# One change to a graph layer: silu and exponentials on ScalarE by other functions, and three other ways to fetch sender rows

## The chip, the cores and the metric

The kernel runs on one core of one Trainium2 chip. The metric is the time of one execution on the device in microseconds. The engines are named as the profile names them: PE (TensorE, matmuls; PEld its weight loads), DVE (VectorE), ACT (ScalarE), POOL (GpSimd), SP (SyncE).

## The reference

One layer of a graph network with attention over all edges: 12500 nodes of 64 features, 412500 edges of 32 features, sorted by receiver.

```python
h = relu(layernorm(x))
msg_in = concat([h[src], h[dst], edge_attr], axis=-1)          # 160 wide
messages = silu(msg_in @ W1 + b1) @ W2 + b2                    # 64 wide
logits = silu(msg_in @ Wa1 + ba1) @ Wa2 + ba2                  # one per edge
att = softmax(logits, axis=0)                                  # over all edges
aggregated = segment_sum(messages * att, dst, num_segments=n)
out = x + silu(concat([h, aggregated]) @ Wu1 + bu1) @ Wu2 + bu2
```

## The kernel before

Head (node stage). `x` is normalised in chunks of 8 or 14 rows per partition; each chunk is transposed into the table `hT` in SBUF and multiplied by two weight blocks. The products are written to DRAM: `ts_d`, the sender table, and then `tr_d`, the receiver table, both 128 wide (64 for attention, 64 for the message), halved so that a tanh can make the silu.

Edge stage. Edges go in 403 groups (`g`) of 8 tiles of 128 edges (`K = 8`). Four groups are a batch for the softmax (fewer at the end). The softmax is kept running: each batch lowers a common maximum `nmax` and the sums so far are scaled. The program order on each engine is written out by hand (`pin`), and each engine works through its instructions in that order. One iteration of the loop over `g` does this:

- `begin(g)`: DVE adds the gathered sender rows `gs` to the receiver and edge part `pe` in PSUM (L553) and ACT takes the tanh of all 1024 columns (L556).
- `sum_up`: the softmax weights and sums of a group some five groups back: ACT copies the segment sums out of PSUM (`ss`, L632), `put` adds them to a table (L651, L655, L658), PE projects, `by_node` builds one-hot weights (`wt`, L620, eight instructions) and multiplies them with the messages.
- `burst`: for every second group from 8 on, one of the 8 tiles isn't gathered. ACT copies its 128 sender columns, four bytes each, out of `hT` at addresses held in registers (L483; the numbers are loaded with L479), 64 a group; PE multiplies that column block by a weight stack (L548), after L547 on DVE has cleared the wrong half.
- `load(g + 2)`: POOL issues 8 or 7 indirect gathers from `ts_d` (L513) into one of seven `gs` buffers. SP loads edge features, receiver numbers and a window of `tr_d` (L524, L527, L534); DVE compares (`eo`, L538) and PE makes `pe` (L542).
- `tile_bias`, in groups 17 to 113 twice in eight groups: PE multiplies a node block and DVE adds a bias (`bu`, L323).
- `end(g)`: DVE completes both silu halves as (tanh + 1) times the input (L566 for messages, L572 for attention), multiplies by `wa2` (L574) and sums (L577). At a batch's end `top` takes the maximum.
- `weigh`: in the first group of the next batch, DVE finds the new maximum (L603, L604, L606) and ACT takes two exponentials (L607, L610).

Behind the loop the sums are divided, the node update runs in 13 tiles and the result is stored.

Of the kernel before, what the change touches and what calls it, by code (L numbers as in the profile page):

```python
# [20 lines left out]
D = 64  # L21
# [21 lines left out]
HT_AT = 4224  # L43
ROUND = 12582912.0
WIDE = 128
EPS = 1e-5
# [11 lines left out]
def gnn_kernel(ctx: ExitStack, tc: tile.TileContext, n_edges, x, src, src_row, dst, dst_row, first, edge,  # L58
# [73 lines left out]
    with tc.tile_pool(name="node1", bufs=1) as node1, \  # L132
# [3 lines left out]

        sizes = [8] + [min(CB, NB - 16 - c) for c in range(0, NB - 16, CB)] + [8] if NB > 16 else [NB]
# [38 lines left out]
        pin(nc.scalar.activation(node1.tile([P, 1], F32, name="spare"), eps, AF.Sqrt))  # L176
        xms, sqs, rstds, hs, tss = ({} for _ in range(5))
# [5 lines left out]
        def subtract(i):  # L183

            n = chunks[i][1]
            total = node.tile([P, CB], F32, name="total")[:, :n]
            pin(nc.vector.tensor_reduce(total, xcs[i], AX.X, ALU.add))
            xm = xms[i] = node.tile([P, CB, D], F32, name="xm", bufs=3)[:, :n, :]
            pin(nc.vector.scalar_tensor_tensor(xm, total[:, :, None].to_broadcast([P, n, D]), -1.0 / D,
                                               xcs[i], op0=ALU.mult, op1=ALU.add))  # L190

        def square(i):
            n = chunks[i][1]
            sq = sqs[i] = node.tile([P, CB, D], F32, name="sq", bufs=3)[:, :n, :]
            pin(nc.scalar.activation(sq, xms[i], AF.Square))

        def totals(i):
            n = chunks[i][1]
            rstd = rstds[i] = node.tile([P, CB], F32, name="rstd")[:, :n]
            pin(nc.vector.tensor_reduce(rstd, sqs.pop(i), AX.X, ALU.add))  # L200
# [4 lines left out]
        def normal(i):  # L205
            n = chunks[i][1]
            rstd = rstds.pop(i)
            pin(nc.vector.reciprocal(rstd, rstd))
# [35 lines left out]
        nch = len(chunks)  # L244
# [22 lines left out]
        for c, nn in chunks:  # L267
# [92 lines left out]
def one_pass(tc, n_edges, v):  # L360
# [17 lines left out]
    with ExitStack() as ctx:  # L378
# [43 lines left out]
        with tc.tile_pool(name="work2", bufs=2) as work2, \  # L422
                tc.tile_pool(name="small", bufs=3) as small, \
                tc.tile_pool(name="pre_ps", bufs=AHEAD + 1, space=PSUM) as pre_ps, \
                tc.tile_pool(name="one_ps", bufs=1, space=PSUM) as one_ps:
            pes, gss, lgs, ps_, psums, sps, pps, ees, mts, nums, cols = ({} for _ in range(11))
# [12 lines left out]
            chosen = {g: i for i, g in enumerate(picks)}  # L439
            hT8 = v["hT"].rearrange("d b p -> d (b p)").bitcast(U8)  # L440
            sets = [(i, min(P, len(picks) - i)) for i in range(0, len(picks), P)]
# [3 lines left out]
            def places():  # L445
# [4 lines left out]
                for k, (i, n) in enumerate(sets):  # L450
                    e = (picks[i] * K + K - 1) * EP
                    nc.sync.dma_start(num[:n, k, :], bass.AP(
                        tensor=v["src_row"].tensor, offset=v["src_row"][:, e:].offset,
                        ap=[[EVERY * K * EP, n], [1, EP]]))
# [8 lines left out]
                for k, (i, n) in enumerate(sets):  # L463
                    nc.sync.dma_start(par_d[k * P:k * P + n, :], low[:n, k, :])
# [3 lines left out]
            def numbers(g):  # L468
                if g in chosen:
                    n = nums[g] = small.tile([P, EP], I32, name="half", bufs=3)  # L470
                    row = par_d[chosen[g]:chosen[g] + 1, :]
                    nc.sync.dma_start(n, bass.AP(tensor=row.tensor, offset=row.offset, ap=[[0, P], [1, EP]]))
                    cols[g] = small.tile([P, EP], F32, name="cols", bufs=3)

            def columns(g, first, n):
                if g not in chosen:
                    return
                to, i = cols[g].bitcast(U8), chosen[g]
                _, regs = nc.values_load_multi_w_load_instructions(  # L479
                    spots[i % P:i % P + 1, i // P, first:first + n], engines=[ENG.Activation],  # L480
                    min_val=HT_AT, max_val=HT_AT + 2 * NP - 4, skip_runtime_bounds_check_because=WHY)
                for i in range(n):
                    pin(nc.scalar.copy(to[:, 4 * (first + i):4 * (first + i) + 4],  # L483
                                       hT8[:, bass.ds(regs[i] - HT_AT, 4)]))

            def burst(g, k):
# [6 lines left out]
            tr_w = bass.AP(tensor=tr_d.tensor, offset=tr_d.offset,  # L493
                           ap=[[C, NP + WR - SHIFT], [SHIFT * C, 2], [1, C]])

            def registers(g, engine, at, base=base_sb, top=NP - 1):
                n = min(NQ, NG + (base is not base_sb) - g)
# [6 lines left out]
            def load(g):  # L504

                t = g * K
                if g % NQ == 0:
                    registers(g, ENG.SP, at_sp)
# [24 lines left out]
                for r in range(2):  # L533
                    nc.sync.dma_start(win[r * R:(r + 1) * R, :, r, :],  # L534
                                      tr_w[bass.ds(at_sp[g], R), :, :])
# [14 lines left out]
            def begin(g):  # L550

                n = K - (g in chosen)
                pin(nc.vector.tensor_tensor(gss[g][:, :n, :], pes[g][:, :n, :], gss[g][:, :n, :], ALU.add))  # L553
                if n < K:
                    pin(nc.vector.tensor_copy(gss[g][:, n, :], pes[g][:, n, :]))
                pin(nc.scalar.activation(pes[g], gss[g], AF.Tanh))  # L556

            def end(g, then=None):

                s = batch[g]  # L560
                if g == starts[s]:
                    lgs[s] = small.tile([EP, B * K], F32, name="lg")
                gs, th = gss.pop(g), pes.pop(g)

                def message():
                    pin(nc.vector.scalar_tensor_tensor(acts[g % ACTS][:, :, 0:U], th[:, :, U:C], 1.0,  # L566
                                                       gs[:, :, U:C], op0=ALU.add, op1=ALU.mult))

                if g < NG - 1:
                    message()  # L570
                att = th[:, :, 0:U]
                pin(nc.vector.scalar_tensor_tensor(att, th[:, :, 0:U], 1.0, gs[:, :, 0:U],  # L572
                                                   op0=ALU.add, op1=ALU.mult))
# [3 lines left out]
                pin(nc.vector.tensor_reduce(lgs[s][:, k:k + K], att, AX.X, ALU.add))  # L577
# [4 lines left out]
                if g == NG - 1:  # L582
                    message()

            def top(s):

                n = size[s] * K
                lg = lgs[s]
# [10 lines left out]
            def weigh(s):  # L599
# [5 lines left out]
                fall = small.tile([P, 1], F32, name="fall")  # L605
                pin(nc.vector.tensor_tensor(fall, nmax[:, s + 1:s + 2], nmax[:, s:s + 1], ALU.subtract))  # L606
                pin(nc.scalar.activation(scale[:, s:s + 1], fall, AF.Exp))  # L607
                p = ps_[s] = small.tile([EP, B * K], F32, name="p")
                psum = small.tile([EP, 1], F32, name="psum")
                pin(nc.scalar.activation(p[:, :n], lgs.pop(s)[:, :n], AF.Exp, bias=nmax[:EP, s + 1:s + 2],  # L610
                                         accum_out=psum))
                psums[s] = psum

            def by_node(g):
# [4 lines left out]
                for j in range(K):  # L619
                    pin(nc.vector.tensor_scalar(wt[:, j, :], iota_w[:EP, j // H, :],  # L620
                                                dloc[:, g * K + j:g * K + j + 1],
                                                p[:, k + j:k + j + 1],
                                                op0=ALU.is_equal, op1=ALU.mult))
# [94 lines left out]
            for g in range(NG):  # L718
# [6 lines left out]
                begin(g)  # L725
                if more and g < NG - 1:
# [10 lines left out]
                if g + AHEAD < NG:  # L737
                    load(g + AHEAD)
                numbers(g + 6)
# [384 lines left out]
```

## Time and profile before

| | |
|---|---|
| median of 3 runs | 3902.49 us (3900.42 to 3908.46) |
| profiled execution | 3904.89 us, span 3903.1 us |
| mean granted TensorE clock | 0.642 |
| indirect gathers on POOL | 3032, first at 51.7, last at 3846.0 us |
| byte copies on ACT | 24576, from 102.8 to 3711.6 us |
| DMA, mean | 100 GB/s |

Shares of busy time are means over head, loop and tail. Register, semaphore and DMA-issuing instructions aren't counted as busy, so an engine that loads register numbers between its instructions looks idle there, with "issue" as the reason.

### The profile page before, as it was taken

The page shows a single profiled execution, that of the slowest core. Times are in us where ns is not written, and L with a number is a line of the kernel's source. Part 1 is how long each engine was busy: PE and PEld are TensorE (multiplying, and loading weights), DVE is VectorE, ACT ScalarE, POOL GpSimd, SP SyncE. Part 2 cuts the span into 40 slices and gives each one's busy share as a digit, 9 for nine tenths or more (in the row PEclk, how much of TensorE's full clock was granted, in tenths as well). Part 3 has the DMA queues.
Part 4 walks back from the last instruction along what each step waited for, and adds up shares of the span by engine and source line. Part 5 has one row for each costly group of instructions (what it writes and reads, how often), then busy time and mean ns, then how long its engine had stood idle before and what let it go on. Part 6 is the DMA issues. An engine that isn't in the chain of part 4 may idle for free. (4 is left out here: it accounts for less than half of the span.)

```text
span 3903.1 us, 72226 instructions
## 1 busy us (share of the span) xinstructions
PE 2368.6 (61%) x11368; PEld 1927.2 (49%) x11368; DVE 3115.4 (80%) x8929; ACT 2954.1 (76%) x25797; POOL 2888.6 (74%) x3057
## 2 busy tenths in 40 slices
PE   6566656666666666665665656556565565555655
PEld 5454444454445554554444545445444454444545
DVE  6888787878788888887877877778777777877887
ACT  2887777777778888887877777878877878878712
POOL 3777777777777777777777777777777777777774
PEclk8766566666666657666666666666666666666666
DMA  7433334333433333333333333333333333333343
GB/s 280 114 104 94 102 100 106 94 104 99 107 93 97 97 97 91 94 97 94 87 97 85 97 93 89 97 86 97 93 88 97 86 96 91 90 97 86 95 116 86
DMA packets 228304, 391.30 MB, mean 100 GB/s; under 512 B 72369, under 2 KB 155762, under 8 KB 214770
## 3 DMA queue, kind: packets, MB, share of 16 engines
q0 software_dynamic: 97024, 198.90, 19.5%
q1 hardware_dynamic: 130802, 187.73, 17.9%
q14 instruction: 385, 3.15, 0.3%
q8 instruction: 93, 1.52, 0.2%
HBM read 360.52 MB, written 25.82 MB: 99 GB/s over the span
## 5 line engine op out<-in xcount | busy, mean ns | idle before, releaser
L513 POOL DMA_INDIRECT gs<-ts_d,src_sb x3032 | 2871.4, 947 | 973.1 <-issue 844.2
L483 ACT COPY cols<-hT 128x4 uint8 x24576 | 2415.5, 189 | 595.2 <-issue 594.2
L542 PE MATMUL pe<-wins,eo 128*128 128x256 f32 x3224 | 1470.7, 630 | 846.4 <-DVE eo L538 619.9
L542 PEld LDWEIGHTS pe<-wins,eo 128*128 128x128 f32 x3224 | 964.4, 316 | 1145.4 <-DVE eo L538 708.6
L620 DVE TENSOR_SCALAR wt<-iota_w,dloc,p 128x40 f32<-128x40 f32 x3224 | 726.9, 323 | 1.8
L553 DVE TENSOR_TENSOR gs<-pe,gs 128x1024 f32<-128x1024 f32 (+1 forms) x403 | 467.0, 1159 | 325.7 <-DMA gs<-ts_d,src_sb 303.3
L626 PE MATMUL sp<-wt,acts 128*65 128x40 f32 x6448 | 621.9, 268 | 4.6 <-DVE wt L620 3.5
L626 PEld LDWEIGHTS sp<-wt,acts 128*65 128x65 f32 x6448 | 586.0, 183 | 11.4 <-DVE wt L620 6.2
L556 ACT ACTIVATE pe<-gs 128x1024 f32<-128x1024 f32 x403 | 410.6, 1019 | 215.9 <-DVE gs L553 125.3
L637 PEld LDWEIGHTS mt<-ss,w2u 65*128 65x128 f32 x806 | 201.7, 281 | 330.4 <-issue 291.9
L637 PE MATMUL mt<-ss,w2u 65*128 65x40 f32 x806 | 183.7, 322 | 255.5 <-DVE gm L603 221.4
L566 DVE SCALAR_TENSOR_TENSOR acts<-pe,gs 128x512 f32<-128x512 f32 x403 | 277.6, 689 | 21.6 <-ACT pe L556 12.2
L574 DVE TENSOR_TENSOR pe<-pe,w_all 128x512 f32<-128x512 f32 x403 | 281.8, 699 | 13.5
L572 DVE SCALAR_TENSOR_TENSOR pe<-pe,gs 128x512 f32<-128x512 f32 x403 | 280.3, 696 | 10.5
L596 PE MATMUL mt<-ident,mx 128*128 128x128 f32 x107 | 46.7, 437 | 396.4 <-DVE sums L655 375.9
L577 DVE TENSOR_REDUCE lg<-pe 128x8 f32<-128x512 f32 x403 | 276.7, 687 | 10.5
L538 DVE TENSOR_SCALAR eo<-dbs,bj 64x256 f32<-64x256 int32 x806 | 275.5, 371 | 9.2
L596 PEld LDWEIGHTS mt<-ident,mx 128*128 128x128 f32 x107 | 19.2, 179 | 408.3 <-issue 404.5
L658 DVE COPY stand<-nmax 64x40 f32 x806 | 159.0, 197 | 3.4 <-issue 0.3
L547 DVE SCALAR_TENSOR_TENSOR cols<-half,cols 128x128 f32<-128x128 int32 x192 | 67.1, 349 | 100.6 <-ACT cols L483 98.5
L651 DVE SCALAR_TENSOR_TENSOR sums<-sums,scale,mt 64x40 f32 x214 | 54.4, 254 | 110.9 <-PE mt L637 107.4
L548 PEld LDWEIGHTS pe<-stack,cols 128*128 128x128 f32 x384 | 121.7, 317 | 32.5
(126 smaller groups left out, 957.6 us busy)
## 6 DMA issues: line engine op xcount, KB each, us to landing
eo<-in_edge_dram SPq DMA_DIRECT2D x100, 512.0 KB
dbs<-in_dst_row_dram SPq DMA_DIRECT2D x200, 256.0 KB
gs<-ts_d,src_sb POOLq DMA_INDIRECT x3032
wins<-tr_d SPq DMA_DIRECT2D x806, 32.0 KB
half<-par_d SPq DMA_DIRECT2D x192, 64.0 KB
ts_d<-ts SPq DMA_DIRECT2D x5, 896.0 KB
tr_d<-tr SPq DMA_DIRECT2D x5, 896.0 KB
hT_d<-hT SPq DMA_DIRECT2D x7, 448.0 KB
```

Of the source, the lines that this page charges most:

```text
L483: pin(nc.scalar.copy(to[:, 4 * (first + i):4 * (first + i) + 4], hT8[:, bass.ds(regs[i] - HT_AT, 4)]))
L513: nc.gpsimd.indirect_dma_start(out=full[:rows, j, :], out_offset=None, in_=ts_d[:, :], in_offset=bass.IndirectOffsetOnAxis(ap=src_full[:ro ...
L542: pin(nc.tensor.matmul(pe[:, 2 * q:2 * q + 2, :], eo[:, q * EP:(q + 1) * EP], win[:, q // 2, :, :], start=True, stop=q < H - 1 or g not in ...
L553: pin(nc.vector.tensor_tensor(gss[g][:, :n, :], pes[g][:, :n, :], gss[g][:, :n, :], ALU.add))
L556: pin(nc.scalar.activation(pes[g], gss[g], AF.Tanh))
L566: pin(nc.vector.scalar_tensor_tensor(acts[g % ACTS][:, :, 0:U], th[:, :, U:C], 1.0, gs[:, :, U:C], op0=ALU.add, op1=ALU.mult))
L572: pin(nc.vector.scalar_tensor_tensor(att, th[:, :, 0:U], 1.0, gs[:, :, 0:U], op0=ALU.add, op1=ALU.mult))
L574: pin(nc.vector.tensor_tensor(att, att, wa2[:EP, None, :].to_broadcast([EP, K, U]), ALU.mult))
L577: pin(nc.vector.tensor_reduce(lgs[s][:, k:k + K], att, AX.X, ALU.add))
L620: pin(nc.vector.tensor_scalar(wt[:, j, :], iota_w[:EP, j // H, :], dloc[:, g * K + j:g * K + j + 1], p[:, k + j:k + j + 1], op0=ALU.is_equ ...
L626: pin(nc.tensor.matmul(sp, acts[g % ACTS][:, j, :], wt[:, j, :], start=j == 0, stop=j == K - 1))
L637: pin(nc.tensor.matmul(pp, w2u.rearrange("s h u -> s (h u)"), sps.pop(g), start=True, stop=True))
```

## The change

- ACT makes both silu halves directly, from PSUM, in two instructions of 512; DVE's two products go. `gs` isn't written any more: the sum is left in `pe`.
- The exponentials are made from a tanh: ACT takes `t = tanh(x / 32)`, DVE forms `(1 + t) / (1 - t)` and squares it three times, ACT squares once more and sums; DVE makes the factor `scale`.
- In every fourth group from 9 on (96 groups) one more tile isn't gathered: DVE copies its 128 columns out of `hT`, 16 in each half of an iteration, with register numbers loaded on DVE.
- In every eighth group from 15 on (47 groups) one more tile isn't gathered: SP fetches its 128 rows of `ts_d` one by one, 16 a group, into `lone`, and DVE adds them apart.
- The first four groups (`FILL = 4`) aren't gathered from `ts_d`: in the head POOL gathers their rows of `x` (32 gathers), which are normalised and multiplied there (`filled`) into `gs` buffers.
- `by_node` makes the weights in two instructions of 320 columns; window addresses are kept in bytes, multiplied beforehand.

On DVE, the order around the exponentials of a batch's first group is: maximum, two scalings, the 16 copies in hand, then `d`, the reciprocal, the product, three squarings, `scale`, then the add of the next group. On ACT, `t` and `p` stand behind both bursts of that group and ahead of the next group's silu.

```diff
+        early = node1.tile([P, FILL * K], I32, name="early")
+        nc.sync.dma_start(early, src[:, :FILL * K])
+        xes = [node1.tile([P, K, D], F32, name=f"xe{g}") for g in range(FILL)]
+        for g in range(FILL):
+            for j in range(K):
+                nc.gpsimd.indirect_dma_start(
+                    out=xes[g][:, j, :], out_offset=None, in_=x[:, :],
+                    in_offset=bass.IndirectOffsetOnAxis(ap=early[:, g * K + j:g * K + j + 1], axis=0))
...
+        def filled(i):
+            h = hs.pop(i)
+            pt = node_ps.tile([P, 4, P], F32, name="pt")
+            for k in range(K // 2):
+                pin(nc.tensor.transpose(pt[:, k, :], h[:, 2 * k:2 * k + 2, :], ident))
+            he = node.tile([2 * D, K // 2, P], F32, name="he")
+            pin(nc.scalar.copy(he, pt))
+            gs = gather.tile([P, K, C], F32, name="gs")
+            ...
+            ready.append(gs)
...
+        squares(nch)
+        for i in range(FILL):
+            totals(nch + i)
+            deviation(nch + i)
+            if i + 1 < FILL:
+                subtract(nch + i + 1)
+                square(nch + i + 1)
+            if i > 0:
+                filled(nch + i - 1)
+            for c in chunks[i * nch // FILL:(i + 1) * nch // FILL]:
+                receivers(*c)
+            normal(nch + i)
+        filled(nch + FILL - 1)
...
+            vpicks = [g for g in range(VSTART + VLATER, NG - 12) if g % VTURN in VRES]
...
+            def vcolumns(g, part):
...
+                    loads, regs = spots_of(t, first, n, ENG.DVE)
+                    for one in loads:
+                        pin(one)
+                    to = cols[t].bitcast(U8)
+                    waiting.extend((to[:, 4 * (first + i):4 * (first + i) + 4], regs[i]) for i in range(n))
+                    at += n
+
+            def spare_columns(n=None):
+                for to, reg in waiting[:n]:
+                    pin(nc.vector.tensor_copy(to, hT8[:, bass.ds(reg - HT_AT, 4)]))
+                waiting[:] = waiting[len(waiting) if n is None else n:]
...
+            def fetch(g):
+                at = (g - ROW0) * ROWS
+                end = min(at + ROWS, len(order) * EP)
...
+                    loads, regs = nc.values_load_multi_w_load_instructions(
+                        ids[i][0:1, first:first + n], engines=[ENG.SP], min_val=0, max_val=(NP - 1) * 4 * C,
+                        skip_runtime_bounds_check_because=WHY)
...
+                    for k in range(n):
+                        pin(nc.sync.dma_start(to[first + k:first + k + 1, :].bitcast(U8),
+                                          ts8[bass.ds(regs[k], 4 * C)][None, :]))
...
-                full = gather.tile([P, K, C], F32, name="gs")
+                full = v["ready"][g] if g < FILL else gather.tile([P, K, C], F32, name="gs")
-                for j in range(K - (g in chosen)):
+                for j in range(K - (g in chosen) - (g in fetched) if g >= FILL else 0):
...
             def begin(g):
-                n = K - (g in chosen)
-                pin(nc.vector.tensor_tensor(gss[g][:, :n, :], pes[g][:, :n, :], gss[g][:, :n, :], ALU.add))
-                if n < K:
-                    pin(nc.vector.tensor_copy(gss[g][:, n, :], pes[g][:, n, :]))
-                pin(nc.scalar.activation(pes[g], gss[g], AF.Tanh))
+                n = K - (g in chosen) - (g in fetched)
+                pe, gs = pes[g], gss.pop(g)
+                pin(nc.vector.tensor_tensor(pe[:, :n, :], pe[:, :n, :], gs[:, :n, :], ALU.add))
+                if g in fetched:
+                    pin(nc.vector.tensor_tensor(pe[:, n, :], pe[:, n, :], lone.pop(g)[:EP], ALU.add))
+                del pes[g]
+                att = atts[g] = silus.tile([P, K, U], F32, name="att")[:EP]
+                pin(nc.scalar.activation(att, pe[:, :, 0:U], AF.Silu, scale=2.0))
+                pin(nc.scalar.activation(acts[g % ACTS][:, :, 0:U], pe[:, :, U:C], AF.Silu, scale=2.0))
...
             def weigh(s):
...
-                fall = small.tile([P, 1], F32, name="fall")
-                pin(nc.vector.tensor_tensor(fall, nmax[:, s + 1:s + 2], nmax[:, s:s + 1], ALU.subtract))
-                pin(nc.scalar.activation(scale[:, s:s + 1], fall, AF.Exp))
+                lg = lgs.pop(s)
+                pin(nc.vector.tensor_scalar(lg[:, n:n + 1], nmax[:, s:s + 1], -1.0, None, op0=ALU.mult))
+                part = small.tile([P, 1], F32, name="part")
+                pin(nc.vector.tensor_scalar(part, nmax[:, s + 1:s + 2], 1.0 / 32, None, op0=ALU.mult))
+                t, d = (small.tile([P, B * K + 1], F32, name=k)[:, :n + 1] for k in ("t", "d"))
+                pin(nc.scalar.activation(t, lg[:, :n + 1], AF.Tanh, bias=part, scale=1.0 / 32))
+                spare_columns()
+                pin(nc.vector.tensor_scalar(d, t, -1.0, 1.0, op0=ALU.mult, op1=ALU.add))
+                spare_columns(3)
+                pin(nc.vector.reciprocal(d, d))
+                spare_columns(3)
+                pin(nc.vector.scalar_tensor_tensor(t, t, 1.0, d, op0=ALU.add, op1=ALU.mult))
+                for _ in range(3):
+                    spare_columns(3)
+                    pin(nc.vector.tensor_tensor(t, t, t, ALU.mult))
                 p = ps_[s] = small.tile([EP, B * K], F32, name="p")
                 psum = small.tile([EP, 1], F32, name="psum")
-                pin(nc.scalar.activation(p[:, :n], lgs.pop(s)[:, :n], AF.Exp, bias=nmax[:EP, s + 1:s + 2],
-                                         accum_out=psum))
+                pin(nc.scalar.activation(p[:, :n], t[:EP, :n], AF.Square, accum_out=psum))
+                spare_columns(3)
+                pin(nc.vector.tensor_tensor(scale[:, s:s + 1], t[:, n:n + 1], t[:, n:n + 1], ALU.mult))
...
             def by_node(g):
-                for j in range(K):
-                    pin(nc.vector.tensor_scalar(wt[:, j, :], iota_w[:EP, j // H, :],
-                                                dloc[:, g * K + j:g * K + j + 1],
-                                                p[:, k + j:k + j + 1],
-                                                op0=ALU.is_equal, op1=ALU.mult))
+                at = dloc[:, g * K:(g + 1) * K].rearrange("p (r h) -> p r h", h=H)
+                pin(nc.vector.tensor_tensor(wt.rearrange("p (r h) w -> p r h w", h=H),
+                                            iota_w[:EP, :, None, :].to_broadcast([EP, 2, H, W]),
+                                            at[:, :, :, None].to_broadcast([EP, 2, H, W]), ALU.is_equal))
+                pin(nc.vector.tensor_tensor(wt, wt, p[:, k:k + K, None].to_broadcast([EP, K, W]), ALU.mult))
...
                 begin(g)
+                vcolumns(g, 0)
...
                     load(g + AHEAD)
+                fetch(g)
                 numbers(g + 6)
...
+                spare_columns()
+                vcolumns(g, 1)
                 end(g)
                 burst(g, 1)
                 if batch[g] and g == starts[batch[g]]:
                     weigh_upto(batch[g] - 1)
+                spare_columns()
```

More of the change, by code (lines that the diff above doesn't have):

```diff
@@ L43 @@
 HT_AT = 4224
+FILL = 4
 ROUND = 12582912.0
 WIDE = 128
+ROWS = 16
+ROW0 = 6
+VTURN = 4
+VRES = (1,)
+VSTART = 3
+VLATER = 6
+VBUFS = 2
 EPS = 1e-5
@@ L425, in one_pass @@
                 tc.tile_pool(name="one_ps", bufs=1, space=PSUM) as one_ps:
[L426 removed]
+            pes, gss, atts, lgs, ps_, psums, sps, pps, ees, mts, nums, cols = ({} for _ in range(12))
             w2t_ps = one_ps.tile([P, 4, P], F32, name="mt")[:U, 0, :S1]
@@ L484, in columns @@
                                        hT8[:, bass.ds(regs[i] - HT_AT, 4)]))
+            waiting = []
+            def vcolumns(g, part):
+                at, end = (i * EP * len(VRES) // (2 * VTURN) for i in (2 * (g - VSTART) + part,
+                                                                        2 * (g - VSTART) + part + 1))
+                end = min(end, len(vpicks) * EP)
+                while 0 <= at < end:
+                    t, first = vpicks[at // EP], at % EP
+                    n = min(end - at, EP - first)
+                    if first == 0:
+                        cols[t] = small.tile([P, EP], F32, name="vcols", bufs=VBUFS)
+                    loads, regs = spots_of(t, first, n, ENG.DVE)
[8 more added lines that the diff above has]
+                waiting[:] = waiting[len(waiting) if n is None else n:]
             def burst(g, k):
@@ L488, in burst @@
                     columns(g + 3 + i, *SLOTS[EVERY - 1 - i][k])
-            at_sp, at_lo, at_hi, bus, rest = {}, {}, {}, {}, {}
[L493 to L497, printed above, removed]
+            fetched = {}
+            for i in range(NG):
+                g = ROW0 + (EP * (i + 1) - 1) // ROWS + 2
+                if g < NG - 12:
+                    fetched[g] = i
@@ new lines, in one_pass, with ask, scaled @@
+            order = list(fetched)
+            ids, lone = {}, {}
+            ts8 = ts_d.rearrange("n f -> (n f)").bitcast(U8)
+            def ask(i):
+                if i < len(order):
+                    g = order[i]
+                    e = (g * K + K - 1 - (g in chosen)) * EP
+                    ids[i] = small.tile([1, EP], I32, name="ids", bufs=2)
+                    nc.sync.dma_start(ids[i], v["src_row"][:, e:e + EP])
+            def scaled(i):
+                if i < len(order):
+                    pin(nc.vector.tensor_scalar(ids[i], ids[i], 9, None, op0=ALU.logical_shift_left))
@@ L561, in end @@
                 if g == starts[s]:
[L562 to L573, printed above, removed]
+                    lgs[s] = small.tile([P, B * K + 1], F32, name="lg")
+                    if EP < P:
+                        pin(nc.vector.memset(lgs[s][P - R:], 0.0))
+                att = atts.pop(g)
                 pin(nc.vector.tensor_tensor(att, att, wa2[:EP, None, :].to_broadcast([EP, K, U]),
```

97 lines of the change are left out of this document (68 added, 29 removed).

## The prediction

> **What bounds the kernel now.** I read the page's table of engines first, then the groups by line, then the first and last starts of single lines, then the timeline. A group is 1024 edges (8 tiles of 128); there are 403, and four make a batch.
>
> ```profile
> PE 2368.6 (61%) x11368; PEld 1927.2 (49%) x11368; DVE 3115.4 (80%) x8929; ACT 2954.1 (76%) x25797; POOL 2888.6 (74%) x3057
> ```
> ```profile
> L513 POOL DMA_INDIRECT gs<-ts_d,src_sb x3032 | 2871.4, 947 | 973.1 <-issue 844.2 <-DMA ts_d<-ts 49.3 <-DMA gs<-ts_d,src_sb 34.8
> L483 ACT COPY cols<-hT 128x4 uint8 x24576 | 2415.5, 189 | 595.2 <-issue 594.2
> ```
> ```profile
> L513 POOL DMA_INDIRECT gs<-ts_d,src_sb x3032: 940/944/1352, 51.7 to 3846.0; - x190
> ```
>
> POOL has the lowest share of the three, yet it is the bound. Its gathers take 2871.4 us and cost 973.1 - 49.3 = 923.8 us of gaps that are nearly all "issue": (2871.4 + 923.8) / 3032 = 1.252 us each, and 3032 x 1.252 = 3795 us is the whole stretch from 51.7 to 3846.0. Before it lie 51.7 us of head, behind it 57.1 us of tail. At 7.5 gathers a group POOL needs 9.39 us a group, 37.6 a batch.
>
> The second engine matters more here. Where POOL's gathers lie ahead in their buffers, ScalarE runs alone:
>
> ```profile
> 1414.30 3.14 ACT L483 COPY cols<-hT 128x4 uint8 x32 [0.92 <-issue]
> 1417.34 0.20 ACT L607 ACTIVATE scale<-fall 128x1 f32<-128x1 f32 x1
> 1417.45 0.31 ACT L610 ACTIVATE p<-lg,nmax 128x32 f32<-128x32 f32 x1
> ...
> 1417.75 1.01 ACT L556 ACTIVATE pe<-gs 128x1024 f32<-128x1024 f32 x1
> ...
> 1426.17 1.02 ACT L556 ACTIVATE pe<-gs 128x1024 f32<-128x1024 f32 x1
> 1427.58 3.14 ACT L483 COPY cols<-hT 128x4 uint8 x32 [0.27 <-issue]
> 1431.64 3.14 ACT L483 COPY cols<-hT 128x4 uint8 x32 [0.92 <-issue]
> 1434.69 1.02 ACT L556 ACTIVATE pe<-gs 128x1024 f32<-128x1024 f32 x1
> ...
> 1443.24 1.02 ACT L556 ACTIVATE pe<-gs 128x1024 f32<-128x1024 f32 x1
> ```
>
> (Columns: start, length, engine, line, result, count, idle before and what ended it.) From tanh to tanh go 8.42, 8.52 and 8.55 us, 8.50 in the mean, with no wait for another engine: two bursts of 32 byte copies, two loads of register numbers, the tanh and a small copy. The two exponentials of a batch (1417.34 to 1417.75) add 0.41. So ScalarE needs 4 x 8.50 + 0.41 = 34.4 us a batch, 3.2 under POOL.
>
> **The change, part by part.** POOL loses one gather in every fourth group from group 9 on (96), one in every eighth (47) and the 32 of the first four groups: 175 x 1.252 = 219 us. The 32 are gathered from x in the head instead, where POOL waited 49.3 us for the sender table: 32 x 1.252 = 40 us, covered. At 7.125 gathers a group POOL would need 8.92 us, 35.7 a batch. If nothing else came up, that would be the result.
>
> VectorE loses the two silu products, the copy of the eighth tile and the eight small weight instructions:
>
> ```profile
> L620 DVE TENSOR_SCALAR wt<-iota_w,dloc,p 128x40 f32<-128x40 f32 x3224 | 726.9, 323 | 1.8
> L574 DVE TENSOR_TENSOR pe<-pe,w_all 128x512 f32<-128x512 f32 x403 | 281.8, 699 | 13.5
> L572 DVE SCALAR_TENSOR_TENSOR pe<-pe,gs 128x512 f32<-128x512 f32 x403 | 280.3, 696 | 10.5
> L566 DVE SCALAR_TENSOR_TENSOR acts<-pe,gs 128x512 f32<-128x512 f32 x403 | 277.6, 689 | 21.6 <-ACT pe L556 12.2
> ```
>
> That is (280.3 + 277.6) / 403 = 1.38 us and 726.9 / 403 = 1.80 us a group; the weights come back as two operations of 320 elements, by L574 (699 ns for 512) some 0.5 and 0.4, 0.9 together. It gains 32 copies of four bytes a group and two loads of 16 register numbers.
>
> ```profile
> 2002.42 0.18 DVE L655 TENSOR_TENSOR sums<-sums,mt 64x40 f32 x1
> 2002.52 0.17 DVE L658 COPY stand<-nmax 64x40 f32 x1
> ```
> ```profile
> L498 DVEq TENSOR_LOAD <-bases x202: 336/343/600, 142.4 to 3853.0; - x101
> L479 ACTq TENSOR_LOAD <-spots x768: 1942/2008/2800, 98.4 to 3706.6; - x192
> ```
>
> Independent small operations start 0.10 apart at 40 elements, though each lasts 0.17; at about 1 ns an element (L574's slope at most) four elements leave 0.06. I take 0.07, range 0.06 to 0.10: 32 x 0.07 = 2.2 us. [...] A load of 4 numbers takes VectorE's queue 0.34 us, one of 32 takes ScalarE's 2.0, so 16 take about 1.1, of which I leave 0.25 bare behind the add and 0.7 behind the weights. An ordinary group then is: add 1.0, load 0.25, four table updates 0.7, two comparisons 0.6, column product 0.3, weights 0.9, copies 1.1, load 0.7, attention product and sum 1.4, copies 1.1: 8.0 us, below ScalarE's 8.5. That VectorE stays below is what hides the copies; at 0.10 a copy it would be 9.0, and they would show.
>
> ScalarE's two silu calls of 512 replace a tanh of 1024. The load of register numbers that runs beside them (the 1.41 us from 1426.17 to 1427.58) hides the second start, so 0.
>
> What decides is the exponential. The tanh form needs, between ScalarE's `t` and ScalarE's `p`, six dependent VectorE operations, then `scale`, and only behind these in VectorE's order comes the next group's add, on which the next silu waits. In the program's order `t` stands behind both bursts of the batch's first group, so VectorE comes to the wait early (about 6.8 us into the group, against 8.5) and cannot hide the chain behind its copies.
>
> ```profile
> 2017.39 0.19 DVE L589 TENSOR_TENSOR lg<-lg,w_all 128x32 f32<-128x32 f32 x1
> 2017.61 0.19 DVE L594 TENSOR_REDUCE mx<-lg 128x1 f32<-128x32 f32 x1
> 2020.44 1.09 DVE L553 TENSOR_TENSOR gs<-pe,gs 128x896 f32<-128x896 f32 x1 [2.64 <-DMA gs<-ts_d,src_sb]
> ```
> ```profile
> L208 DVE RECIPROCAL rstd<-rstd 128x14 f32<-128x14 f32 x5 | 1.2, 239 | 2.0 <-ACT rstd L203 1.9
> L208 DVE RECIPROCAL rstd<-rstd 128x8 f32<-128x8 f32 x2 | 0.4, 196 | 1.3 <-ACT rstd L203 1.3
> ```
>
> `t` 0.30 (L610, nearly the same size); a dependent operation of 32 elements 0.22 (2017.39 to 2017.61), of which there are five with the first a little shorter: 1.1; the reciprocal of 33, at 43 ns for six more elements, 0.38 + 0.03; `scale` and hand-overs 0.15; the add 1.09. That is 3.05 us from `t` to the next silu, where 0.41 stood. The bounds: 2.3, if each small one took 0.15, to 3.5.
>
> Once a silu has waited, ScalarE's load of register numbers starts late too:
>
> ```profile
> 2012.66 1.03 ACT L556 ACTIVATE pe<-gs 128x1024 f32<-128x1024 f32 x1 [0.56 <-DVE gs L553]
> 2013.62 0.18 ACT L632 COPY ss<-sp 65x40 f32<-65x40 f32 x1
> 2014.78 3.14 ACT L483 COPY cols<-hT 128x4 uint8 x32 [0.97 <-issue]
> ```
>
> 2.12 us from tanh to copies instead of 1.41: 0.7 more. A batch is then 4 x 8.50 + 3.05 + 0.7 = 37.75 us, 9.44 a group, with POOL waiting at its 35.7.
>
> In the stretch with the node-bias tiles VectorE also waits for TensorE in every fourth group, the one behind the chain:
>
> ```profile
> 663.74 1.23 DVE L553 TENSOR_TENSOR gs<-pe,gs 128x1024 f32<-128x1024 f32 x1 [0.21 <-issue]
> ...
> 665.65 0.62 DVE L538 TENSOR_SCALAR eo<-dbs,bj 64x256 f32<-64x256 int32 x2
> ...
> 666.88 1.01 ACT L556 ACTIVATE pe<-gs 128x1024 f32<-128x1024 f32 x1
> ...
> 670.73 0.98 DVE L323 TENSOR_SCALAR bu<-mt,w_all 64x256 f32<-64x256 f32 x2 [4.46 <-PE mt L314]
> ...
> 671.88 1.77 DVE L620 TENSOR_SCALAR wt<-iota_w,dloc,p 128x40 f32<-128x40 f32 x8
> ```
> ```profile
> L553 DVE TENSOR_TENSOR gs<-pe,gs x403: 1072/1205/1226, 96.4 to 3849.8; 128x1024 f32<-128x1024 f32 x71, 128x896 f32<-128x896 f32 x64
> L323 DVE TENSOR_SCALAR bu<-mt,w_all x50: 341/477/490, 235.8 to 1173.6; 64x256 f32<-64x256 f32 x48, 64x128 f32<-64x128 f32 x2
> L483 ACT COPY cols<-hT x24576: 176/189/196, 102.8 to 3711.6; 128x4 uint8 x200
> ```
>
> Today VectorE begins that group's add 3.1 us before ScalarE's tanh (663.74, 666.88) and absorbs part of the wait; after the chain it has no lead. From the end of the add to the weights go 671.88 - 663.74 - 1.23 = 6.9, then load 0.25, weights 0.9, copies 1.1, load 0.7, attention 1.4, copies 1.1, add 1.1: 13.5 us. The batch: 11.55 (8.50 + 3.05) + 13.5 + 9.2 + 8.5 = 42.8, where today's is (1173.6 - 235.8) / 24 = 39.1.
>
> The sum, on the profiled execution (span 3903.1, 3904.9 with what lies around it, 2.4 above the median of the three runs). To the first bias tile 235.8 + 14 = 250: four early groups cost VectorE four more normalisations (four 512-element passes of 0.7 each, 11 us, of which I let 8 show), and three chains cost 6 beyond slack. The bias stretch, 24 batches: 1027. Then to the last byte copy (group 387), 68.6 batches x 37.75 = 2588, today 3711.6 - 1173.6 = 2538. The last stretch is 191.5 us today, 138 of them for 14 groups to the last add (3849.8), at POOL's 8 gathers or 10 us a group; with seven buffers filled ahead they go at VectorE's pace without copies, 8.0 - 2.2 - 0.95 for the loads and about 2.5 for a softmax step in nearly each, 7.4 us, so 34 less: 157. Together 4022; with 1.8 around it and less the 2.4, **4020 us**.
>
> **The rivals.** *The gathers stay the bound (chance 0.14), on the other side: faster.* This needs the batch of ScalarE and VectorE under 35.7 us, so chain and late load under 1.7 instead of 3.75, the add alone being 1.09. Then: 24 gathers fill the three free buffers before the first add at 96.4 + 8, about 105 us, 2833 x 1.252 = 3547, tail 57: 3709, some 3710 us. For it speaks that VectorE's copies may make it so late that `t` is done already; against it, that lateness on VectorE delays the add as well. A detail can raise it:
>
> ```profile
> 417.25 0.68 DVE L355 TENSOR_TENSOR xt<-xt,w_all 128x512 f32<-128x512 f32 x1
> 417.42 1.33 POOL L513 DMA_INDIRECT gs<-ts_d,src_sb  x1 [0.30 <-issue]
> ```
>
> A gather begun 0.17 into an operation with two SBUF operands took 1.33 instead of 0.94. The attention product becomes such an operation (it read PSUM). Meeting at random, one of 0.7 costs about 0.55 x 0.55 / 2 / 1.25 = 0.12 us a group: 3760. [...]
>
> *SyncE becomes the bound (0.06).* It issues 16 more one-row transfers a group.
>
> ```profile
> L534 SPq DMA_DIRECT2D wins<-tr_d x806: 316/317/1870, 88.2 to 3808.7; - x162
> ```
>
> 16 x 0.32 = 5.1, 1.0 for loading 16 numbers, about 2 for what it issues now: 8 us of 9.44. It decides above 0.41 an issue; at 0.45 a group is 10.1, 370 x 0.7 = 250 us more: 4270.
>
> *VectorE's copies cost their whole 0.17 us (0.05):* 3.2 us more a group, 11.2 in three of four groups; about 4800. *The terms cancel and the time stays within 0.2% (0.04).*
>
> **How the numbers follow.** 0.2%, 8 us, is about what a measurement can tell from no change. The forecast has 0.71 and is slower; with SyncE and VectorE 0.81 slower, 0.15 faster (0.14 for POOL, 0.01 for the forecast's lower edge), 0.04 same. Its own range: the chain at 2.3 and no late load take off 1.45 x 92 batches, 133 us: 3885; copies at 0.10 add 1.0 a batch and 2.0 in a bias batch, 117: 4140. The range is these two.
>
> **What would show it.** Right: ScalarE's longest waits are the silu for VectorE's add and `p` for the squares, once a batch, 2.5 us together; silu to silu 11.5 us in a batch's first group and 8.5 in its last; gathers waiting for buffers, POOL busy under 70%. Wrong: gathers still end the waits of L690 and POOL's gaps stay at 0.30; or `t` starts before the second burst; or copies on VectorE more than 0.10 apart; or SyncE issuing without a gap.

## The result and the profile after

The changed kernel takes 4166.19 us (4163.72 to 4169.27), the kernel before 3901.9 (3900.42 to 3908.46): a ratio of 1.0674, interval 1.0656 to 1.0693. Slower was forecast, 4020 us, from 3885 to 4140; the 264 us of loss are more than twice the 118 forecast, and the time lies 26 us above the range.

From the page of the changed kernel, the engines and some groups by line:

```profile
PE 2336.4 (56%) x11608; PEld 1936.5 (46%) x11608; DVE 3332.0 (80%) x18868; ACT 2983.4 (72%) x26221; POOL 2828.3 (68%) x2914
...
L649 POOL DMA_INDIRECT gs<-ts_d,src_sb x2857 | 2773.2, 971 | 1268.1 <-issue 758.3
...
L695 ACT ACTIVATE att<-pe 128x512 f32<-128x512 f32 x403 | 237.9, 590 | 277.4 <-DVE pe L690 269.2
...
L742 DVE TENSOR_SCALAR d<-t 128x33 f32<-128x33 f32 (+2 forms) x107 | 22.8, 213 | 222.4 <-ACT t L740 222.3
...
L752 ACT ACTIVATE p<-t 128x32 f32<-128x32 f32 (+2 forms) x107 | 24.3, 227 | 169.3 <-DVE t L749 169.3
```

POOL isn't the bound any more: its gaps hold 410 us beyond the usual 0.30 a gather (1268.1 less 2857 x 0.30). ScalarE and VectorE wait for each other instead: the silu (L695) for the add (L690), `d` for `t`, `p` for the squares. One batch in the timeline, from the add of its first group to that of the next batch (start, length, engine, line, result, count, idle before and what ended it):

```profile
2212.43 1.10 DVE L690 TENSOR_TENSOR pe<-pe,gs 128x896 f32<-128x896 f32 x1
...
2212.79 5.36 SPq L618 DMA_DIRECT2D lone<-ts_d  x16
...
2213.93 0.58 ACT L695 ACTIVATE att<-pe 128x512 f32<-128x512 f32 x1
...
2215.69 3.14 ACT L545 COPY cols<-hT 128x4 uint8 x32 [0.62 <-issue]
2216.00 1.26 DVE L568 COPY vcols<-hT 128x4 uint8 x16
...
2219.76 3.14 ACT L545 COPY cols<-hT 128x4 uint8 x32 [0.92 <-issue]
2222.80 0.32 ACT L740 ACTIVATE t<-lg,part 128x33 f32<-128x33 f32 x1
2223.16 0.31 DVE L742 TENSOR_SCALAR d<-t 128x33 f32<-128x33 f32 x1 [2.17 <-ACT t L740]
2223.50 0.36 DVE L744 RECIPROCAL d<-d 128x33 f32<-128x33 f32 x1
2223.90 0.19 DVE L746 SCALAR_TENSOR_TENSOR t<-t,d 128x33 f32<-128x33 f32 x1
2224.13 0.65 DVE L749 TENSOR_TENSOR t<-t 128x33 f32<-128x33 f32 x3
2224.82 0.23 ACT L752 ACTIVATE p<-t 128x32 f32<-128x32 f32 x1 [1.69 <-DVE t L749]
2224.82 0.16 DVE L754 TENSOR_TENSOR scale<-t 128x1 f32<-128x1 f32 x1
...
2225.12 1.10 DVE L690 TENSOR_TENSOR pe<-pe,gs 128x896 f32<-128x896 f32 x1
2226.26 0.60 ACT L695 ACTIVATE att<-pe 128x512 f32<-128x512 f32 x1 [1.12 <-DVE pe L690]
...
2228.38 2.29 ACT L545 COPY cols<-hT 128x4 uint8 x23 [0.97 <-issue]
```
```profile
2233.18 1.10 DVE L690 TENSOR_TENSOR pe<-pe,gs 128x896 f32<-128x896 f32 x1
...
2239.89 0.25 DVE L794 SCALAR_TENSOR_TENSOR sums<-sums,scale,mt 64x40 f32 x1 [0.76 <-PE mt L780]
...
2251.18 1.08 DVE L690 TENSOR_TENSOR pe<-pe,gs 128x896 f32<-128x896 f32 x1
```

The forecast mechanism is there: VectorE waits 2.17 us for `t` before it can start `d`, and from `t` to the next silu go 3.46 us. The silu-to-silu time of this group is 12.33, of which 8.87 lie before `t`.

Two rows, the first and last starts of the bias operation and of the byte copies, cut the span into the stages of the prediction:

```profile
L377 DVE TENSOR_SCALAR bu<-mt,w_all x50: 343/477/491, 267.8 to 1339.4; 64x256 f32<-64x256 f32 x48, 64x128 f32<-64x128 f32 x2
...
L545 ACT COPY cols<-hT x24576: 187/189/219, 129.5 to 4005.3; 128x4 uint8 x200
```

| stage | before | forecast | after |
|---|---|---|---|
| to the first bias tile, us | 235.8 | 250 | 267.8 |
| batch in the bias stretch (24), us | 39.1 | 42.8 | 44.65 |
| batch behind it (68.6), us | 37.0 | 37.75 | 38.86 |
| from the last byte copy to the end, us | 191.5 | 157 | 160.3 |

The excess over the forecast is 18 + 24 x 1.85 + 68.6 x 1.11 + 3 = 142 us of the 4165.6 us span. The direction of every stage was right. So were most of the signs named beforehand: the two waits of ScalarE (1.69 and 1.12 us above) come to 2.8 us a batch where 2.5 was named, and POOL, waiting for buffers, is busy 68%. A batch's first group takes 12.3 us from silu to silu, not the 11.5 named (mean of 66 batches behind the bias stretch).

### The profile page after: what moved, and what is told of

The parts are those of the page before. It is cut to its first block, busy times and chain, and to the rows that moved or that the text cites. A ratio compares the mean times of both kernels' runs of the same rounds, so it can differ in the third digit from the quotient of the medians.

```text
span 4165.6 us, 94121 instructions
## 1 busy us (share of the span) xinstructions
PE 2336.4 (56%) x11608; PEld 1936.5 (46%) x11608; DVE 3332.0 (80%) x18868; ACT 2983.4 (72%) x26221; POOL 2828.3 (68%) x2914
## 5 line engine op out<-in xcount | busy, mean ns | idle before, releaser
L649 POOL DMA_INDIRECT gs<-ts_d,src_sb x2857 | 2773.2, 971 | 1268.1 <-issue 758.3
L568 DVE COPY vcols<-hT 128x4 uint8 x12288 | 978.5, 196 | 77.6 <-issue 77.2
L769 PE MATMUL sp<-wt,acts 128*65 128x40 f32 x6448 | 561.8, 256 | 29.1 <-DVE wt L766 29.1
L690 DVE TENSOR_TENSOR pe<-pe,gs 128x896 f32<-128x896 f32 (+1 forms) x403 | 453.6, 1125 | 26.2 <-PE pe L678 5.2
L695 ACT ACTIVATE att<-pe 128x512 f32<-128x512 f32 x403 | 237.9, 590 | 277.4 <-DVE pe L690 269.2
L706 DVE TENSOR_TENSOR att<-att,w_all 128x512 f32<-128x512 f32 x403 | 279.2, 693 | 165.3 <-issue 150.7
L709 DVE TENSOR_REDUCE lg<-att 128x8 f32<-128x512 f32 x403 | 275.0, 682 | 10.4
L696 ACT ACTIVATE acts<-pe 128x512 f32<-128x512 f32 x403 | 235.1, 583 | 0.0
L766 DVE TENSOR_TENSOR wt<-wt,p 128x320 f32<-128x320 f32 x403 | 198.5, 493 | 13.9
L763 DVE TENSOR_TENSOR wt<-iota_w,dloc 128x320 f32<-128x320 f32 x403 | 194.5, 483 | 0.1
```

Source lines behind the costliest of these rows:

```text
L568: pin(nc.vector.tensor_copy(to, hT8[:, bass.ds(reg - HT_AT, 4)]))
L649: nc.gpsimd.indirect_dma_start(out=full[:rows, j, :], out_offset=None, in_=ts_d[:, :], in_offset=bass.IndirectOffsetOnAxis(ap=src_full[:ro ...
L690: pin(nc.vector.tensor_tensor(pe[:, :n, :], pe[:, :n, :], gs[:, :n, :], ALU.add))
L695: pin(nc.scalar.activation(att, pe[:, :, 0:U], AF.Silu, scale=2.0))
L696: pin(nc.scalar.activation(acts[g % ACTS][:, :, 0:U], pe[:, :, U:C], AF.Silu, scale=2.0))
L706: pin(nc.vector.tensor_tensor(att, att, wa2[:EP, None, :].to_broadcast([EP, K, U]), ALU.mult))
```

## The experiments

The kernels ran in five sets, each beside the kernel before. In three sets the kernel before itself took 5847, 5883 and 5862 us; these sets are called disturbed here, and their times aren't compared with those of the other two (kernel before 3901.8 and 3902.6). What was slow in them stands under the hardware below. A number at the end of a name means that the kernel had run before in a disturbed set. Stage times come from the same two rows in each kernel's trace, in us:

| kernel | us | first bias tile | bias batch | batch behind it | end |
|---|---|---|---|---|---|
| after_again | 4166.26 | 264.9 | 44.67 | 38.86 | 159.8 |
| no_fetch | 4153.03 | 264.8 | 44.69 | 38.67 | 160.7 |
| no_fill | 4146.19 | 244.8 | 44.74 | 38.83 | 161.2 |
| no_chain3 | 4004.06 | 260.5 | 43.12 | 37.30 | 145.2 |
| no_vcopies3 | 4025.01 | 259.7 | 40.25 | 38.42 | 161.0 |
| move_chain3 | 4139.13 | 268.8 | 44.48 | 38.51 | 160.2 |
| move_all | 4028.07 | 246.2 | 40.94 | 38.47 | 160.1 |

**Control: the changed kernel again.**

> The changed kernel itself, beside the kernel before, as a control: in the two sets so far the kernel before took 5847 and 5883 us and the byte copies had gaps of about 0.7 us. If this set is like those: theory 1 puts it between bias_early and no_chain's 5547 plus the 160 us of the chain, 5700 to 5780, so faster than the kernel before there. If the copies run closely again: 4166 beside 3902.

4166.26 us beside 3901.8, ratio 1.0681 (1.0663 to 1.0699): the first result, repeated.

**Without SyncE's rows.** The tiles that SyncE fetched row by row are gathered.

```diff
-                if g < NG - 12:
+                if False:
                     fetched[g] = i
```

> The 47 tiles fetched by SyncE row by row are gathered again (7.25 gathers a group, 9.08 us, 36.3 a batch). Theory 1: nobody waits for SyncE's rows, so within 20 us of the changed kernel (4166 where the copies run closely, about 5750 where they don't). If SyncE's 6016 issues or their data hold the kernel up: 100 us or more faster.

4153.03 us, 13 less than the changed kernel. SyncE doesn't hold the kernel up. With its rows go VectorE's extra add in every eighth group and the shift of the row numbers; the silu-to-silu time of the group with the extra add, behind the bias stretch, falls from 8.88 to 8.53 us in the mean of 33.

**Without the early groups.** `FILL = 0`, and all receivers are computed in one pass behind `windows()`.

> The first four groups are gathered from the sender table again; the head does nothing for them. The first add came 24 us later with the change (120.7 against 96.4 us). If all of that is the four groups made in the head: 20 to 25 us less than the changed kernel. If the 32 gathers, 40 us of POOL, come on the path instead: no gain or a loss of up to 16 us.

4146.19 us, 20 less; the first add comes at 95.5 instead of 118.1 us. The kernel before has its first add at 96.4, so the whole delay of the first add was the four groups made in the head.

**Without the chain's operations.** `p` and `scale` are squares of `t` itself, so the softmax weights are other numbers.

```diff
                 spare_columns()
-                pin(nc.vector.tensor_scalar(d, t, -1.0, 1.0, op0=ALU.mult, op1=ALU.add))
-                ...
-                    pin(nc.vector.tensor_tensor(t, t, t, ALU.mult))
                 p = ps_[s] = small.tile([EP, B * K], F32, name="p")
```

> Leaves out the six VectorE operations between `t` and `p` (other softmax weights). Theory 1: 1.75 us a batch less, the chain group 10.5 instead of 12.3 us, 92 x 1.75 = 160 us: 4005. What stays against move_chain3 is `t`, `scale` and the add in series. Theory 2: the same 1.75 us, but then move_chain3 gains nothing.

4004.06 us. From `t` to the next silu go 1.81 us instead of 3.36 (means of 66 batches behind the bias stretch), and the batch falls by 1.56, close to the 1.75 expected; the time is the 4005 expected.

**Without VectorE's copies.** `VRES = ()`; the 96 tiles are gathered.

> The 96 tiles copied by VectorE are gathered again: 36.9 us a batch for POOL, 3.5 to 4 us a group less for VectorE. Theory 1: ScalarE's path is untouched, 38 to 38.9 us a batch, 4080 to 4170. Theory 2: the gathers' 36.9, 3985.

4025.01 us, which lies between the times of the two theories; but the batch behind the bias stretch falls only from 38.86 to 38.42, where theory 1 had 38 to 38.9 and theory 2 had 36.9. From the timeline of no_vcopies3:

```profile
2101.96 0.32 ACT L740 ACTIVATE t<-lg,part 128x33 f32<-128x33 f32 x1
2102.32 0.18 DVE L742 TENSOR_SCALAR d<-t 128x33 f32<-128x33 f32 x1 [5.34 <-ACT t L740]
...
2103.88 0.16 DVE L754 TENSOR_TENSOR scale<-t 128x1 f32<-128x1 f32 x1
...
2104.26 1.23 DVE L690 TENSOR_TENSOR pe<-pe,gs 128x1024 f32<-128x1024 f32 x1 [0.21 <-DMA gs<-ts_d,src_sb]
...
2105.52 0.60 ACT L695 ACTIVATE att<-pe 128x512 f32<-128x512 f32 x1 [1.32 <-DVE pe L690]
```

VectorE now waits 5.34 us for `t`, with nothing else to do, and the silu still comes 3.56 us behind `t`: there the loss is the chain, not VectorE's load. Of the 141 us, 24 x 4.4 = 106 come from the bias stretch, where the group behind the chain is VectorE's: its silu-to-silu time falls from 13.0 to 10.0 us (means of the second and sixth group of each eight).

**The chain moved behind the next add.**

```diff
                 begin(g)
+                for s in later:
+                    chain(s)
                 vcolumns(g, 0)
                 if more and g < NG - 1:
                     next(more)
+                while later:
+                    powers(later.pop())
```

(`weigh` ends with `t`; `chain` holds `d` to `scale`, `powers` holds `p`.)

> The kernel of move_chain once more, beside a kernel before of 3902 us if the copies run closely. Theory 1 (the wait for `t`, the chain and the add in series before the next silu): 36 to 36.5 us a batch in place of 38.9, the group of the chain 9 in place of 12.3 us, 3900 to 3950. Theory 2 (VectorE's load, wherever the chain stands): within 40 us of 4166.

4139.13 us: 27 less, not 240. That is theory 2's number, VectorE's load; but with that load taken away instead (no_vcopies3) the batch stayed at 38.42, which is theory 1's. Neither theory is enough alone. The timeline of move_chain3 shows the silu's wait gone, and what came in its place:

```profile
2173.02 0.32 ACT L740 ACTIVATE t<-lg,part 128x33 f32<-128x33 f32 x1
2173.25 0.57 ACT L695 ACTIVATE att<-pe 128x512 f32<-128x512 f32 x1
2173.38 0.43 DVE L747 TENSOR_SCALAR d<-t 128x33 f32<-128x33 f32 x1 [1.09 <-ACT t L740]
...
2175.16 0.23 ACT L760 ACTIVATE p<-t 128x32 f32<-128x32 f32 x1 [0.78 <-DVE t L751]
...
2176.50 0.19 DVE L804 TENSOR_TENSOR sums<-sums,mt 64x40 f32 x1 [1.19 <-issue]
...
2177.19 3.14 ACT L545 COPY cols<-hT 128x4 uint8 x32 [1.71 <-issue]
```

The silu stands right behind `t` (0.23 us instead of 3.46). But VectorE, early now, waits 1.09 us for `t`, and its numbers, loaded behind that wait, come 1.19 us late; ScalarE's `p` waits 0.78, and its load of 32 numbers, which stands behind `p` in its queue, leaves the copies waiting 1.71 us instead of 0.97. The waits of ScalarE over the same stretch, 1400 to 3900 us, first of the changed kernel, then of move_chain3 (total, times, longest):

```profile
ACT cols L545 <- issue: 389.9, 515, 1.3
...
ACT p L752 <- DVE t L749: 103.5, 65, 1.8
ACT att L695 <- DVE pe L690: 72.5, 66, 1.5
```
```profile
ACT cols L545 <- issue: 510.2, 520, 2.0
...
ACT p L760 <- DVE t L751: 39.9, 65, 0.8
...
ACT att L695 <- DVE pe L690: 1.6, 6, 0.5
```

Of 134 us won at silu and `p`, 120 are lost again to late register numbers. Not all of that is `p`'s place in the queue: in the batch's other three groups, too, the copies come 1.5 to 2.1 us behind the silu (means of 33 to 65 groups), because VectorE's add ends there only 0.1 to 0.7 us before it. With VectorE over 4 us ahead (no_vcopies3) it is 1.34.

**Chain moved, bias matmul ahead, no early groups.** TensorE's matmul of the bias tile is issued ahead of `load` in that iteration, VectorE's operation stays.

```diff
+                early_bias = iter(())
+                if g >= 16 and g // 8 - 2 < NT and g % 8 in (1, 5):
+                    early_bias = tile_bias(...)   # a generator now
+                    next(early_bias, None)        # the matmul
                 burst(g, 0)
                 ...
-                if g >= 16 and g // 8 - 2 < NT and g % 8 in (1, 5):
-                    tile_bias(...)
+                for _ in early_bias:              # VectorE's part
+                    pass
```

> Three edits together: the chain behind the next add, the node-bias matmul ahead of the loads of its iteration, and the first four groups gathered from the sender table again (20 us, measured). Theory 1: 36 to 36.5 us a batch in the steady stretch, 36.5 to 37.5 in the bias stretch in place of 44.7, so 4166 - 20 - 170 - 180 = about 3800, within 40, faster than the kernel before by 2 to 3%. If another wait comes in the bias stretch: 3850 to 3930.

4028.07 us, neither 3800 nor 3850 to 3930: the bias stretch gains 3.5 us a batch, the stretch behind it nothing more. VectorE's wait for that matmul, of the changed kernel and of move_all (260 to 1340 us):

```profile
DVE bu L377 <- PE mt L368: 104.1, 25, 4.5
```
```profile
DVE bu L376 <- PE mt L366: 12.6, 23, 0.7
```

So the matmul's place is worth 4139.13 - 20 - 4028.07 = 91 us, if the 20 us of the early groups simply add. Within one disturbed set the same edit, on the kernel with the chain moved, was worth 98 us (5422.7 and 5324.65); alone it gave 5660, with no changed kernel beside it in that set:

> TensorE's matmul of the node-bias tile is put ahead of the eight `pe` matmuls of the load in that iteration instead of behind them; VectorE's operation stays where it is. In 25 groups, each the one behind a chain, VectorE waits 4.2 us there for TensorE, 104 us in all. If that wait, with no lead on VectorE behind the chain, is what makes these groups 13 us long: they fall to 9.3 to 9.8 and the time by 80 to 95 us, to 4070 to 4085. If something else of those groups sets them (the chain before, or `pe` coming later by the 0.8 us of the matmul): less than 30 us.

> The chain behind the next add, and the matmul of the node-bias tile ahead of the loads of its iteration. In 25 groups VectorE waited 4.2 us for that matmul. Theory 1: with the chain moved VectorE has some lead there, so part of the 4.2 us is gone already; the matmul ahead takes the rest, 40 to 100 us under move_chain2: 3820 to 3890, and the stretch of the bias tiles at 36 to 37.5 us a batch. If these groups are long for another reason: as move_chain2.

**What can't be read.** move_chain, move_chain2, no_chain, no_vcopies and no_vcopies2 were earlier runs, in disturbed sets, of kernels shown above (5421, 5423, 5547, 6142, 6153 us beside 5847 to 5883). Three kernels ran only there:

> Only ScalarE's silu and the tanh form of the exponentials, the weights in two operations and the window addresses in bytes; gathers as before (no columns on VectorE, no rows by SyncE, no groups gathered in the head). Theory 1: the batch is the larger of the gathers' 37.6 us and ScalarE's 38 to 38.9: 3.5 to 5% above no change in the edge stage less the 24 us of the head, 3960 to 4130, so the loss is in this part alone. Theory 2 (loss from VectorE's copies or SyncE's rows): 3902 or less, as the gathers bound it at 37.6.

> move_all without VectorE's copies (those 96 tiles gathered again; 2985 gathers). If chain and VectorE's load are two bounds side by side: both are gone and the gathers bind, 52 + 2985 x 1.252 + 57 = 3846 us, 36.9 a batch, gathers with gaps of 0.30 and no waits for buffers; 3830 to 3870, faster than the kernel before. If a third thing holds the batch at 38.4: 3950 to 4000.

> Bias matmul ahead, early groups from the sender table, VectorE copies one tile in eight groups instead of one in four (8 columns in each half of an iteration), and the chain in another place: the maximum and `t` ahead of the second burst of the batch's first group, the VectorE operations behind that group's attention product, `p` behind the second burst, so that neither engine waits. 2937 gathers. If the two bounds are all: VectorE needs 34 us a batch, ScalarE 34.6, the gathers 36.3, and 52 + 2937 x 1.252 + 57 = 3786 us; with some loss where VectorE comes late, 3780 to 3830, the fastest of all. If a third thing holds it: 3950 to 4000.

6190.63 us (ratio 1.0511), 5779.07 (0.9859) and 6051.02 (1.0341). Of the 265 groups from 120 to 384, 62 to 77% had gaps of their own within the byte copies, and no two groups in a row were without, so none of the three settles its question. Whether the gathers would bind again, at some 3850 us, with the chain moved and VectorE's copies gone is open; no version that ran undisturbed beats the kernel before.

> The kernel before with a profile, to see what makes 5850 us of 3902 in these sets. If it is the byte copies alone: the gathers keep their 0.944 and 0.30 us and wait for buffers, and ScalarE's idle time behind `issue` rises from 594 us by about as much as the time does, some 1900. If the gathers themselves or the DMA are slower, their 947 ns rise.

before_again ran in an undisturbed set: 3902.01 us.

## Why the prediction was right in direction and wrong in size

**The bound.** POOL stopped being the bound and the chain `t` to the next silu took its place, as forecast: without the chain's operations the batch is 37.30 us (no_chain3), and with the chain but without VectorE's copies still 38.42 (no_vcopies3). What wasn't forecast is a second bound of the same size, VectorE's load and the register loads that come late with it: with the silu's wait gone the batch is still 38.51 (move_chain3). The rivals are out. The gathers wait for buffers; SyncE's issues took 0.335 us each (16 in 5.36 us, below the 0.41 that would decide) and no_fetch won 13 us; sixteen of VectorE's copies took 1.26 us, (1.26 - 0.16) / 15 = 73 ns apart, where 70 were taken. An ordinary group of VectorE's took 8.06 us from add to add (2225.12 to 2233.18) where 8.0 was summed.

**The mis-sized terms behind the bias stretch, 1.1 us a batch or 76 us.** In the means of 66 batches: silu to `t` 8.94 us, not 8.50; `t` to silu 3.36, not 3.05 (in the batch shown `d` took 0.34 to the next start where 0.2 stood, and from `scale` to the add go 0.30, where 0.15 stood for `scale` and all hand-overs); the late load 0.82 (9.32 less 8.50), not 0.7; the groups of SyncE's rows 0.35 in every second batch, counted as nothing. The first, the largest, is the step that failed: 4 x 8.50. The 8.50 us was taken as ScalarE's own need in a group whatever VectorE does, but was read where VectorE was far ahead. The numbers of the first burst are loaded in ScalarE's queue behind the silu's wait for the add. In the timeline above the add ends at 2213.53, 0.4 us before the silu; the load, 2.0 us long, starts at 2213.65, and the copies come 1.76 us behind the silu instead of 1.41:

```profile
L535 ACTq TENSOR_LOAD <-spots x1: 1969/1969/1969, 2213.7 to 2213.7; - x1
```

The chain's groups of 65 batches agree: the load starts 0.12 us behind the add's end, the add ends 0.43 us before the silu, and the copies come 1.77 us behind it. In the batch's third groups, where the add ends 1.33 us before the silu, they come at 1.35. Without VectorE's copies, the add 4.8 us ahead, silu to `t` is 8.50 again.

**The bias stretch, 1.85 us a batch or 45 us.** The long group behind the chain was summed right (13.5 forecast, 13.0 measured), but the chain's own group took 12.9 instead of 11.55, the third 9.4 instead of 9.2 and the batch's last 9.2 instead of 8.5. The same step failed here: silu to `t` is 9.1 us, and 8.5 without VectorE's copies; the last group, too, is 8.5 without them. `t` to silu is 3.75, but 3.3 to 3.5 in 20 of the 24 batches; in three of the other four 14 to 20 byte copies run in between, which the sum didn't have.

**The start, 18 us.** Four early groups were let show with 8 us; they cost 20 (no_fill). That is 12 of the 18; the cause of the rest is open.

**The cover.** "That VectorE stays below is what hides the copies" held for an ordinary group, not for a batch. From 2212.43 to 2251.18, one batch of VectorE's, 38.75 us, less 2.17 and 0.76 of waits, its work is 35.8 us; ScalarE's is 4 x 8.50 + 0.55 = 34.6. With two engines this close, each waiting for the other once a batch, neither was hidden behind the other. The 36 us a batch expected of the moved chain left that out as well. Whether lifting both bounds together gives those 36 us isn't shown, since moved_no_vcopies ran disturbed.

## What to carry to other kernels

Price a dependent chain between two engines by everything that queues behind each of its waits, register loads too: moved elsewhere, the wait came back here as late loads (120 of the 134 us won). When two engines are within a few per cent of each other, sum both over the whole period with its rare steps, not over the ordinary iteration. A gain on the engine that binds (6% of POOL's gathers) was worth nothing here, because the next bound, ScalarE and VectorE together, didn't stay below it. A time read as one engine's own need holds only with the lead of the other engines under which it was read (here 8.50 us with VectorE ahead, 8.94 without).

## What the runs showed of the hardware

In the disturbed sets many of ScalarE's byte copies, 0.095 us apart otherwise, stood 0.4 to 1.5 us apart, and nearly all of these while gathers were being issued. From scalar_alone (gathers as in the kernel before):

```profile
2214.73 2.38 ACT L543 COPY cols<-hT 128x4 uint8 x24
2214.89 0.95 POOL L647 DMA_INDIRECT gs<-ts_d,src_sb  x1 [0.30 <-issue]
...
2217.39 0.94 POOL L647 DMA_INDIRECT gs<-ts_d,src_sb  x1 [0.31 <-issue]
2217.43 0.19 ACT L543 COPY cols<-hT 128x4 uint8 x1 [0.32 <-issue]
2218.14 0.19 ACT L543 COPY cols<-hT 128x4 uint8 x1 [0.52 <-issue]
...
2219.55 0.29 ACT L543 COPY cols<-hT 128x4 uint8 x2 [1.21 <-issue]
```

Of the 23,800 steps from copy to copy within its bursts, those over 0.3 us are at most 0.1% where no more than two gathers started in the last 6 us, 6% at three, 23% at four and 42% at five. In before_again it is 5 steps of 23,800, though four in five of its steps had five gathers in the 6 us; one chip ran in both kinds of set. The gathers themselves kept a median of 0.94 to 0.95 us. What differs between those times isn't shown by any trace here.

Gathers that begin within a VectorE operation with two SBUF operands last longer, in the median 1.01 us against 0.94 for the others, as the prediction's row suggested:

```profile
2245.29 0.49 DVE L766 TENSOR_TENSOR wt<-wt,p 128x320 f32<-128x320 f32 x1
2245.51 1.08 POOL L649 DMA_INDIRECT gs<-ts_d,src_sb  x1 [0.30 <-issue]
```

It ends 0.81 us behind the operation; the median of the long ones is 0.82, wherever in the operation they began. 340 of 2857 gathers lasted 1.0 us or more (52 of 3032 before), and 314 of the 340 began within such an operation, of 524 that did; of the 2333 others 26 lasted as long. POOL isn't the bound here, and what the longer gathers cost in time wasn't measured.
